# Cross-attention on one core: probability casts behind two score tiles in the filling slots, last value stores on GpSimd's queue, and the last normalization and value pass moved in the end

## The chip, the cores and the metric

The kernel runs on one core of one Trainium2 chip. The metric is the device time of one execution in microseconds (us). Before the change it is 1960.85 us, the median of 3 runs (1959.88 to 1962.95).

## What is computed

The reference, cut to what matters. `x` is (32, 512, 640), `ctx_2048` is (32, 77, 1024), all float32, 20 heads of 32 columns. The other three attention branches of the reference read context rows beyond the 77th, of which there are none, so they add nothing.

```python
q = _heads(hidden_states @ to_q_w)
p = softmax(einsum('bhqd,bhkd->bhqk', q, k) / sqrt(32))   # k = _heads(ctx @ to_k_w)
h_txt = einsum('bhqk,bhkd->bhqd', p, v)                   # v = _heads(ctx @ to_v_w)
out = _merge(h_txt) @ to_out_w + to_out_b + residual
```

## The kernel before, in words

Every float32 operand of a matmul is split into a high part (a cast to float32r, on ScalarE, ACT in the profile) and a low part (a subtraction on VectorE, DVE, or on GpSimd, POOL), and each product is three matmuls on TensorE (PE): high by high, high by low, low by high.

**Stages.** First the keys and values of all 32 x 77 context rows are computed in groups of 512 rows and stored in DRAM as `k_dram` and `v_dram`. The last group has 416 rows (group `LAST`); its values are still being computed while the main loop begins. Then come 160 slots, one for each tile n = 5b + j of batch b and chunk j of four heads. At the end the function `end` closes the last batch.

**A slot.** Slot n does, in the order in which `slot` (lines 660 to 762) writes it down, the scores and exponentials of tile n (four score tiles t of 128 queries, each into one of 3 banks `sc`, with a maximum `nm` on DVE, line 461, and four ACT exponentials with their sums, line 471), the queries of tile n+1 (`pq`, line 434, split into `qt` by line 103 on ACT and line 104 on DVE), the normalization of tile n-1 (`rs`, line 481 on DVE; `pn`, line 486 on POOL), its transposition (`z`, line 493 on DVE), the stores of `z` to DRAM (four DMAs `pd`, line 500), the load of tile n-2 in the layout that the value pass needs (`raw`, two DMAs, lines 509 and 510), and the value pass of tile n-3: `cast_p` (line 517, ACT, 128x1024), `rest_p` (line 523, ACT, 64x512, and line 524, DVE, 128x1024), `last_p` (line 531, POOL, 64x512), six matmuls `pa` (line 545), `sum_a` (line 556 on ACT into `aw`, two sums in line 558 on DVE), and one slot later `high_a` (line 565, ACT) and `low_a` (line 570, DVE), which give `at`. The output projection of an earlier batch (`po`, line 588, in pieces that `piece` deals out) and its sum with bias and residual (`finish`, line 617, DVE, and a DMA) fill the rest of PE's time.

**What sets the order.** Each engine works its instructions off in the order of the program text; nothing is rescheduled. A DMA waits in the queue of the engine that issues it (SP for nearly all), and keeps what is behind it waiting. A tile with one buffer (`z`, `pp`, `aw`, `pa`) or two or three (`raw`, `sc`, `po`) is written again only when its last reader is done; for `z` that is the landing of the four `pd` stores.

**Filling slots.** A slot is called filling if it has a value pass (n of 3 and more) but no output projection yet: slots 3 to 6. In slots 0 and 1 the last value chunks of group `LAST` are computed beside the scores: chunks 0 and 1 come ahead of slot 0, chunk 2 in slot 0, chunks 3 and 4 in slot 1. `split_values` (line 221) writes them to one of two buffers `vs` and stores each with four DMAs on SP (line 233).

**The end.** In slot 159 nothing is ahead. Its last lines take the value pass of tile 156 with `take` (line 641: `values`, `sum_a`, `high_a`, `low_a`). `end` (line 764) then takes tiles 157, 158 and 159 (N-3, N-2, N-1), normalizes tile 159, transposes, stores and loads it, and begins eight output banks of the last batch: banks 0 to 2 are `sc` banks, 3 the `pq` bank, 4 and 5 the `po` banks, 6 and 7 halves of the `pa` bank. `begin(i, j0, j1)` adds the products of chunks j0 to j1-1 to bank i, three matmuls each, and `close(t)` adds chunk 4, which needs the `at` of the last tile, to the two banks of row tile t and finishes them.

Of the kernel before, what the change touches and what calls it, by code (L numbers as in the profile page):

```python
# [51 lines left out]
def kernel(  # L52
# [25 lines left out]
    nc = tc.nc  # L78
# [8 lines left out]
    N = B * NC_  # L87
# [133 lines left out]
    def split_values(g, j, between=None):  # L221

        g0, gn = GROUPS_KV[g]
        na = gn // Q
        vs = vss[j % 2]
        vt = vs[:, :na, 2].bitcast(F32)
        nc.vector.transpose(vt, pvs.pop(j)[:, :gn].rearrange("p (a d) -> p a d", d=HD))
        if between is not None:
            between()
        split(vs[:, :na, 0], vs[:, :na, 2], vt)  # L230
        dst = v_dram[g0 : g0 + gn, :, j].rearrange("(a t) i c d -> i t a (c d)", t=Q)
        for i in range(HPC):
            nc.sync.dma_start(
                dst[i].bitcast(F32),
                vs[i * Q : (i + 1) * Q, :na].rearrange("p a c d -> p a (c d)").bitcast(F32),
            )
# [73 lines left out]
    LAST, split_ks = len(GROUPS_KV) - 1, []  # L310
# [155 lines left out]
    def exps(n, t, sc, nm):  # L466
        if t == 0:
            sms[n] = main.tile([P, NQ * HPC], F32, tag="sm", name="sm", bufs=2)
        for i in range(HPC):
            at = t * HPC + i  # L470
            nc.scalar.activation(  # L471
                pnb[n % 2][:, at, :NKEY],
                sc[:, i * NKEY : (i + 1) * NKEY],
                AF.Exp,
                bias=nm[:, i : i + 1],
                accum_out=sms[n][:, at : at + 1],
            )
# [133 lines left out]
    def finish():  # L611

        while closed:
            b, t, h = closed.pop(0)
            xr = xrs[b, t]
            cols = slice(h * HALF, (h + 1) * HALF)
            nc.vector.tensor_tensor(  # L617
                xr[:, cols], pos.pop((b, t, h))[:, :HALF], xr[:, cols], ALU.add
            )
            if (b, t) == (B - 1, NQ - 1):  # L620
                nc.sync.dma_start(out[b, t * P : (t + 1) * P, cols], xr[:, cols])
            elif h == 1:
                nc.sync.dma_start(out[b, t * P : (t + 1) * P, :], xr)
# [17 lines left out]
    def take(m):  # L641
        values(m)
        sum_a(m)
        high_a(m)
        low_a(m)
# [14 lines left out]
    def slot(n, beside=()):  # L660
        b, j = divmod(n, NC_)
        ahead, more = n + 1 < N, b + 1 < B
        back, first = PIECES[j]
        bo_, has_out = b - back, b >= back
        xsplits = SPLIT_X.get(j, ((), ())) if more and n > LATE else ((), ())
        turns = TRANSPOSE_X.get(j, ((), (), ())) if more and b else ((), (), ())
        if b == 1 and j < 2:
            turns = (((), (), ()), ((0, 1), (2,), ()))[j]
        taken = takes.get(n)

        filling = taken is not None and not has_out
        if not filling:
            refill(b, j, 0)
        if taken is not None:
            cast_p(taken)
        if n - 1 in takes:
            high_a(takes[n - 1])
        s = scores(n, 0)
        if taken is not None:
            rest_p(taken)  # L680
        rs = sums(n - 1) if n else None
        if taken is not None:
            last_p(taken)
        if n:
            normalize(n - 1, rs)
        if n - 1 in takes:
            low_a(takes[n - 1])
        exps(n, 0, *s)
        if ahead:
            queries(n + 1, 0, 2)  # L690
        s = scores(n, 1)
        if n - LAG + 1 in pds and n > LATE:
            load_p(n - LAG + 1)
        if filling:
            refill(b, j, 0)
        if n == NC_:
            load_x(b + 1, (2, 3))
        for k in WO.get(n, ()):
            nc.sync.dma_start(wos[0][:, k].bitcast(F32), wo_dram[:, k].bitcast(F32))
        refill(b, j, 1)  # L700
        finish()
        if j == 4 and b and b + 2 < B:
            load_x(b + 2, (0, 1))
        if j in RESIDUAL and b >= RESIDUAL[j][0]:
            load_residual(b - RESIDUAL[j][0], RESIDUAL[j][1])
        if j in BIAS and b >= BIAS[j][0]:
            add_bias(b - BIAS[j][0], BIAS[j][1])
        exps(n, 1, *s)
        for i in turns[0]:
            transpose_x(b + 1, i)  # L710
        if ahead:
            queries(n + 1, 2, NC_)
        s = scores(n, 2)
        if not ahead:
            exps(n, 2, *s)
            piece(bo_, first)
            s = scores(n, 3)
        if j == 3 and has_out:
            piece(bo_, first)
            finish()  # L720
        if n and has_out:
            transpose_p(n - 1)
        if ahead:
            split_q(n + 1)
            exps(n, 2, *s)
        if n and not has_out:
            transpose_p(n - 1)
        if j == 4 and b + 2 < B:
            load_x(b + 2, (0, 1) if not b else (2, 3))
        for c in xsplits[0]:  # L730
            split_x(b + 1, c)
        if not ahead:
            exps(n, 3, *s)
            finish()
            piece(bo_, first + 1)
            take(taken)
            return
        if has_out:
            if j != 3:
                piece(bo_, first)  # L740
        else:
            s = scores(n, 3)
        if taken is not None:
            values(taken)
        if len(beside) > 0:
            context_values(LAST, beside[0], psv)
        if has_out:
            s = scores(n, 3)
        finish()
        for i in turns[1]:  # L750
            transpose_x(b + 1, i)
        if taken is not None:
            sum_a(taken)
        for c in xsplits[1]:
            split_x(b + 1, c)
        exps(n, 3, *s)
        if len(beside) > 1:
            context_values(LAST, beside[1], psv)
        if has_out:
            piece(bo_, first + 1)  # L760
        for i in turns[2]:
            transpose_x(b + 1, i)

    def end():


        last = B - 1
        load_p(N - 2)
        cast_p(N - 3)
        rest_p(N - 3)  # L770
        last_p(N - 3)
        normalize(N - 1, sums(N - 1))
        add_bias(last - 1, 3)
        piece(last - 1, 6)
        finish()
        piece(last - 1, 7)
        finish()
        transpose_p(N - 1)
        load_p(N - 1)
        load_residual(last, 0)  # L780
        load_residual(last, 1)
        piece(last - 1, 8)
        take(N - 3)
        piece(last - 1, 9)
        cast_p(N - 2)
        rest_p(N - 2)
        last_p(N - 2)
        finish()
        spare = late[0].tile([P, 3, S], F32, tag="raw", name="xr", bufs=2)
        load_residual(last, 3, spare.rearrange("p k q -> p (k q)")[:, :C])  # L790
        load_residual(last, 2)

        def begin(i, j0, j1):
            t, h = divmod(i, 2)
            if j0 == 0:
                if i < 3:
                    pos[last, t, h] = ps.tile([P, S], F32, tag="sc", name="po", bufs=3)
                elif i == 3:
                    pos[last, t, h] = ps.tile([P, S], F32, tag="pq", name="po", bufs=1)
                elif i < 6:  # L800
                    output_bank(last, t, h)
                else:
                    if i == 6:
                        pas[N] = late[1].tile([P, 2, S], F32, tag="pa", name="po", bufs=1)
                    pos[last, t, h] = pas[N][:, i - 6]
            for j in range(j0, j1):
                project(last, t, h, j)

        begin(0, 0, 2)
        begin(1, 0, 2)  # L810
        take(N - 2)
        cast_p(N - 1)
        rest_p(N - 1)
        last_p(N - 1)
        for t in (0, 1, 3, 2):
            add_bias(last, t)
        begin(2, 0, 3)
        begin(0, 2, 4)
        begin(1, 2, 4)
        begin(2, 3, 4)  # L820
        for i in range(3, 6):
            begin(i, 0, 4)
        take(N - 1)

        def close(t):
            for h in range(2):
                project(last, t, h, 4)
                closed.append((last, t, h))
            finish()

        begin(6, 0, 4)
        close(0)
        close(1)
        begin(7, 0, 4)
        close(2)
        close(3)

    load_keys(0, 0)
# [63 lines left out]
```

## Time and profile before

| | |
|---|---|
| median of 3 runs | 1960.85 us (1959.88 to 1962.95) |
| the profiled execution: its own time, its span | 1961.89 us, 1959.8 us |
| granted PE clock, mean | 0.992 |
| PE busy | 1909.2 us, 97% of the span |
| ACT, DVE, POOL busy | 78%, 73%, 51% |
| HBM traffic over the span | 219 GB/s |

The span runs from the first to the last instruction; all times within it count from its start. A line of the timeline gives start, duration, engine, line of the kernel, operation, and in brackets how long the engine had been idle ahead of it and what ended that idle time. A line of the windows gives the stretch, its length, the busy time of PE, PEld (weight loads), DVE, ACT and POOL with the number of instructions, the granted PE clock, the busy share of the DMA engines and GB/s. PEq, SPq and the like are the queues of instructions that issue or wait and are not counted as busy. Idle time on an engine that is not the bottleneck costs nothing.

### The profile page before, as it was taken

Reading aid. Unit: us, or ns where it says so; the run is one execution under the profiler, and the core shown is the slowest. Engines: PE = TensorE matmul, PEld = TensorE weight load, DVE = VectorE, ACT = ScalarE, POOL = GpSimd, SP = SyncE. Lnnn points to the kernel's source line nnn. Section 1 sums busy time; section 2 is a strip of 40 time slices with the busy share of each in tenths; the row PEclk is TensorE's granted clock in tenths of the full one; section 3 lists DMA queues with packets and bytes.
Section 4 is the critical chain, followed back from the end, with each engine's and each line's share of the span. In section 5 each row is a group of like instructions: output and inputs, shape, how many; then the busy total and the mean of one; then the engine's idle time right before and its main releaser. Section 6 shows DMA issues by size and latency. Waiting matters only on the chain.

```text
span 1959.8 us, 36241 instructions
## 1 busy us (share of the span) xinstructions
PE 1909.2 (97%) x10332; PEld 1704.8 (87%) x10332; DVE 1436.2 (73%) x2334; ACT 1534.3 (78%) x6210; POOL 1002.3 (51%) x648
## 2 busy tenths in 40 slices
PE   9999997899999999999999999999999999999997
PEld 7787896798988989989999988889989998988896
DVE  4444345778788888888888777787878878878774
ACT  3232237888889888888888888899888988888982
POOL 1000033655566555555556555666556665566643
PEclk9999998999999999999999999999999999999999
DMA  9878869888888888888998888888898888888874
GB/s 187 185 182 234 197 159 238 219 226 226 226 229 234 223 234 232 231 228 222 235 236 230 230 212 238 229 235 223 226 235 231 226 228 226 226 226 228 226 212 135
DMA packets 568279, 431.28 MB, mean 220 GB/s; under 512 B 195344, under 2 KB 477072, under 8 KB 568080
## 3 DMA queue, kind: packets, MB, share of 16 engines
q1 hardware_dynamic: 564848, 417.65, 83.0%
q0 software_dynamic: 3136, 11.14, 1.6%
q8 instruction: 84, 1.38, 0.3%
q14 instruction: 115, 0.94, 0.2%
q10 hardware_dynamic: 96, 0.16, 0.0%
HBM read 247.17 MB, written 181.64 MB: 219 GB/s over the span
## 4 chain that ended last, share of the span: by engine, by line
PE 21%; DMA 19%; issue 17%; ACT 16%; DVE 12%; POOL 11%; SPq 3%; DVEq 0%; POOLq 0%; ACTq 0%
DMA raw<-pd 8%; ACT pn L471 8%; DMA pd<-z 8%; POOL pn L486 7%; PE pq L434 6%; PE po L588 6%; POOL pp L531 3%; DVE pp L524 3%; PE pv L191 3%; PE sc L453 2%; PE pk L191 2%; ACT xt L262 2%; ACT aw L556 2%; DVE nm L461 2%; DVE z L493 2%
## 5 line engine op out<-in xcount | busy, mean ns | idle before, releaser
L471 ACT ACTIVATE pn<-sc,nm 128x77 f32<-128x77 f32 x2560 | 802.6, 335 | 76.6 <-DVE nm L461 74.3
L588 PE MATMUL po<-wo_s,at 128*128 128x320 f32 x3840 | 626.0, 311 | 21.5 <-DVE xr L617 14.2
L434 PE MATMUL pq<-xt,wq_s 128*128 128x512 f32 x2400 | 605.7, 393 | 0.0
L588 PEld LDWEIGHTS po<-wo_s,at 128*128 128x128 f32 x3840 | 576.6, 189 | 32.2 <-DVE xr L617 24.6
L531 POOL TENSOR_TENSOR pp<-raw,pp 64x512 fp32r<-64x512 f32 x160 | 211.1, 1319 | 663.6 <-ACT pp L523 390.4
L471 ACT ACTIVATION_READ_ACCUMULATOR pn<-sc,nm 128x1 f32 x2560 | 545.2, 213 | 0.0
L434 PEld LDWEIGHTS pq<-xt,wq_s 128*128 128x128 f32 x2400 | 437.0, 188 | 75.2
L453 PE MATMUL sc<-kb,qt 128*128 128x308 f32 x1920 | 379.1, 306 | 13.9 <-ACT pn L471 10.4
L486 POOL TENSOR_TENSOR pn<-pn,rs 128x1232 f32<-128x1232 f32 x160 | 364.4, 2278 | 32.9 <-DVE rs L481 20.5
L453 PEld LDWEIGHTS sc<-kb,qt 128*128 128x128 f32 x1920 | 325.5, 189 | 59.3 <-ACT pn L471 12.3
L493 DVE STREAM_TRANSPOSE z<-pn 128x1280 f32<-128x1280 f32 x160 | 241.8, 1512 | 176.1 <-POOL pn L486 166.7
L461 DVE TENSOR_REDUCE nm<-sc 128x4 f32<-128x308 f32 x640 | 294.5, 462 | 41.3 <-PE sc L453 39.2
L524 DVE TENSOR_TENSOR pp<-raw,pp 128x1024 fp32r<-128x1024 f32 x160 | 195.5, 1222 | 91.8 <-ACT pp L517 86.7
L545 PE MATMUL pa<-pp,vb 128*128 128x512 f32 x960 | 253.3, 399 | 1.6 <-DVE pp L524 0.8
L558 DVE TENSOR_TENSOR pa<-pa,aw 64x512 f32<-64x512 f32 x320 | 222.7, 696 | 31.5 <-ACT aw L556 22.2
L263 POOL TENSOR_TENSOR xt<-xs,xt 128x512 fp32r<-128x512 f32 x160 | 204.4, 1296 | 37.8 <-ACT xt L262 36.9
L556 ACT COPY aw<-pa 64x1024 f32<-64x1024 f32 x160 | 162.0, 1013 | 69.5 <-PE pa L545 66.7
L545 PEld LDWEIGHTS pa<-pp,vb 128*128 128x128 f32 x960 | 175.3, 189 | 32.2 <-DVE pp L524 1.1
L517 ACT CAST pp<-raw 128x1024 fp32r<-128x1024 f32 x160 | 168.8, 1055 | 43.2 <-DMA raw<-pd 43.0
L581 POOL TENSOR_TENSOR xr<-xr,bias 128x640 f32<-128x640 f32 x128 | 201.6, 1576 | 0.1
L191 PE MATMUL pk<-ct,wk_s 128*128 128x512 f32 (+1 forms) x600 | 140.5, 394 | 8.2 <-ACT ct L103 6.3
L191 PEld LDWEIGHTS pk<-ct,wk_s 128*128 128x128 f32 x600 | 116.2, 195 | 30.8 <-ACT ct L103 7.2
(42 smaller groups left out, 1347.0 us busy)
## 6 DMA issues: line engine op xcount, KB each, us to landing
pd<-z SPq DMA_DIRECT2D x640, 160.0 KB, 3.9
raw<-pd SPq DMA_DIRECT2D x160, 512.0 KB, 4.0
xs<-in_x_dram SPq DMA_DIRECT2D x128, 320.0 KB, 6.2
xr<-in_x_dram SPq DMA_DIRECT2D x128, 320.0 KB, 4.1
out_dram<-xr SPq DMA_DIRECT2D x127, 320.0 KB, 4.1
raw<-pd SPq DMA_DIRECT2D x160, 128.0 KB, 4.2
v_dram<-vs SPq DMA_DIRECT2D x80, 192.0 KB, 3.9
k_dram<-ks POOLq DMA_DIRECT2D x20, 512.0 KB, 3.4
```

The source lines that it names most:

```text
L191: nc.tensor.matmul(held[j][:, :gn], w[:, k, a, :], cts[g, k][:, c, :gn], start=(k == 0 and n == 0), stop=(k == NK - 1 and n == 2),)
L434: nc.tensor.matmul(pqs[n], wq_s[:, k, a, j * P : (j + 1) * P], xts[b, k][:, c, :], start=(k == 0 and m == 0), stop=(k == NC_ - 1 and m == 2),)
L453: nc.tensor.matmul(sc[:, :KCOLS], qt[:, a, t * P : (t + 1) * P], kb[:, j - GROUPS[g][0], c], start=(m == 0), stop=(m == 2),)
L461: nc.vector.tensor_reduce(nm, sc[:, :KCOLS].rearrange("p (h k) -> p h k", k=NKEY), AX.X, ALU.max, negate=True)
L471: nc.scalar.activation(pnb[n % 2][:, at, :NKEY], sc[:, i * NKEY : (i + 1) * NKEY], AF.Exp, bias=nm[:, i : i + 1], accum_out=sms[n][:, at : ...
L486: nc.gpsimd.tensor_tensor(pf, pf, rs.unsqueeze(2).to_broadcast([P, NQ * HPC, NKEY]), ALU.mult)
L493: nc.vector.transpose(z.rearrange("p b t j -> p t b j"), pn.rearrange("p (t h) k -> p t (h k)", t=NQ).rearrange("p t (b i) -> p t b i", i=Q),)
L524: nc.vector.tensor_tensor(pp[:, 2:4, :], raw[:, 0:2, :], pp[:, 0:2, :].bitcast(F32), ALU.subtract)
L531: nc.gpsimd.tensor_tensor(pp[64:, 4, :], raw[:64, 2, :], pp[:64, 4, :].bitcast(F32), ALU.subtract)
L545: nc.tensor.matmul(pas[n][:, p, :], vb[:, p, t, :], pp[:, c, :], start=(c == p), stop=(t == 1),)
L558: nc.vector.tensor_tensor(pa[64 * p : 64 * p + 64, 0], pa[:64, p], aw[:, p], ALU.add)
L588: nc.tensor.matmul(pos[b, t, h][:, :HALF], ats[b * NC_ + j][:, a, t * P : (t + 1) * P], wos[0][:, j, c, h * HALF : (h + 1) * HALF], start= ...
```

## The change

1. The 20 DMAs that store the values of group `LAST` are issued by GpSimd, no longer by SP. In POOL's queue the stores of chunk 2 stand ahead of the normalization of tile 0, and those of chunks 3 and 4 ahead of that of tile 1.
2. In slots 3 to 6 the casts of the probabilities (`cast_p`, `rest_p`, `last_p`) come after the exponentials of score tiles 0 and 1. On ACT two tiles of exponentials stand ahead of them; on DVE the subtraction `pp` stands behind the reciprocal and the maximum of score tile 1 and ahead of the maximum of score tile 2; on POOL `pp` comes after the normalization.
3. In slot 159 the reciprocal and the normalization of tile 159 come directly after its last exponentials, and `end` begins with the transposition of tile 159 and its four stores, ahead of `high_a` and `low_a` of tile 156. On DVE `z` thus stands ahead of `at`, `pp` and the two sums `xr` that it followed before. On SP its stores stand ahead of an output store. On POOL the normalization comes ahead of `pp` of tile 157.
4. The value pass of the last tile is taken after bank 3, ahead of banks 4 and 5 (24 matmuls); banks 6 and 7, which lie in the `pa` bank, come behind `close(1)` and `close(2)`.

No instruction is added or removed on any engine, apart from the DMAs that change their queue.

```diff
         dst = v_dram[g0 : g0 + gn, :, j].rearrange("(a t) i c d -> i t a (c d)", t=Q)
+        engine = nc.gpsimd if g == LAST else nc.sync
         for i in range(HPC):
-            nc.sync.dma_start(
+            engine.dma_start(
...
-        if taken is not None:
+        if taken is not None and not filling:
             cast_p(taken)
...
         s = scores(n, 0)
-        if taken is not None:
+        if taken is not None and not filling:
             rest_p(taken)
         rs = sums(n - 1) if n else None
-        if taken is not None:
+        if taken is not None and not filling:
             last_p(taken)
...
         exps(n, 1, *s)
+        if filling:
+            cast_p(taken)
+            rest_p(taken)
+            last_p(taken)
         for i in turns[0]:
             transpose_x(b + 1, i)
...
             exps(n, 3, *s)
+            normalize(n, sums(n))
             finish()
             piece(bo_, first + 1)
-            take(taken)
+            values(taken)
+            sum_a(taken)
             return
...
         load_p(N - 2)
+        transpose_p(N - 1)
+        high_a(N - 4)
+        low_a(N - 4)
         cast_p(N - 3)
         rest_p(N - 3)
         last_p(N - 3)
-        normalize(N - 1, sums(N - 1))
         add_bias(last - 1, 3)
...
         finish()
-        transpose_p(N - 1)
         load_p(N - 1)
...
-        for i in range(3, 6):
-            begin(i, 0, 4)
+        begin(3, 0, 4)
         take(N - 1)
+        begin(4, 0, 4)
+        begin(5, 0, 4)
...
-        begin(6, 0, 4)
         close(0)
         close(1)
+        begin(6, 0, 4)
+        close(2)
         begin(7, 0, 4)
-        close(2)
         close(3)
```

## The prediction

> **What bounds the kernel now.** I read the page first (PE busy 97% of 1959.8 us), then the waits of PE by stage, the windows by slot, and the timelines of the two places that the change touches. From 420 to 1900 us PE waits 10.3 us in all, every one for `xr L617`, which the change leaves alone: a steady slot of 10.1 us is PE's. So the loop gives nothing, and what PE loses before and after it is lost for good.
>
> The fill is slots 3 to 7. The windows, one slot each (PE, PEld, DVE, ACT, POOL, clock, DMA share, GB/s):
>
> ```profile
> 304.18:318.03 13.85, 8.76 (x34) 7.06 (x35) 6.16 (x10) 8.82 (x45) 4.01 (x2) 0.82 0.84 219
> 318.03:326.71 8.68, 7.70 (x34) 6.17 (x32) 5.83 (x11) 8.45 (x33) 6.84 (x5) 0.90 0.97 260
> 326.71:338.55 11.84, 7.97 (x34) 6.07 (x34) 7.50 (x12) 9.14 (x42) 4.00 (x3) 0.93 0.78 193
> 338.55:348.49 9.94, 8.42 (x38) 6.65 (x36) 8.65 (x15) 8.77 (x40) 3.57 (x3) 0.91 0.99 204
> 348.49:361.58 13.09, 10.64 (x57) 9.19 (x58) 9.80 (x15) 11.43 (x46) 7.20 (x5) 1.00 0.65 172
> ```
>
> No engine fills slots 3, 5 or 7; slot 4 is ACT's (8.45 of 8.68). The timeline of the fill shows why:
>
> ```profile
> 300.82 5.51 SPq L233 DMA_DIRECT2D v_dram<-vs  x8
> ...
> 306.38 0.52 SPq L509 DMA_DIRECT2D raw<-pd  x1
> ...
> 311.69 1.04 ACT L517 CAST pp<-raw 128x1024 fp32r<-128x1024 f32 x1 [3.68 <-DMA raw<-pd]
> ...
> 314.53 1.14 PE L453 MATMUL sc<-kb,qt 128*128 128x308 f32 x3 [4.90 <-ACT pn L471]
> ...
> 336.11 0.69 PE L453 MATMUL sc<-kb,qt 128*128 128x308 f32 x3 [3.44 <-ACT pn L471]
> ...
> 359.44 1.51 DVE L493 STREAM_TRANSPOSE z<-pn 128x1280 f32<-128x1280 f32 x1 [2.86 <-POOL xr L581]
> ...
> 361.58 0.41 PE L453 MATMUL sc<-kb,qt 128*128 128x308 f32 x1 [2.15 <-DVE qt L104]
> ```
>
> In slot 3 the cast stands in ACT's queue ahead of the exponentials, and waits for a load that SP issued behind eight value stores; PE waits 4.90 us for the bank those exponentials free. In slot 7 the transpose `z` of DVE is late (POOL's `pn` had long ended; the stores `pd` issued from 353.46 for 3.55 us, last out of `z`, are what ended it) and `qt` behind it holds PE 2.15 us.
>
> The timeline of the end:
>
> ```profile
> 1911.95 2.21 SPq L500 DMA_DIRECT2D pd<-z  x4
> ...
> 1917.36 0.38 SPq L509 DMA_DIRECT2D raw<-pd  x1
> ...
> 1917.80 4.19 PE L588 MATMUL po<-wo_s,at 128*128 128x320 f32 x18 [2.97 <-DVE xr L617]
> ...
> 1920.75 1.51 DVE L493 STREAM_TRANSPOSE z<-pn 128x1280 f32<-128x1280 f32 x1 [2.61 <-POOL pn L486]
> ...
> 1941.51 1.56 PE L545 MATMUL pa<-pp,vb 128*128 128x512 f32 x6
> ...
> 1947.03 8.85 PE L588 MATMUL po<-wo_s,at 128*128 128x320 f32 x48 [3.96 <-DVE at L570]
> ```
>
> After the last value pass (1941.51) PE has nothing it may do until `at` is split at 1946.97; 24 matmuls that could run there were run before it.
>
> **Part 1: last values stored by GpSimd.** 20 DMAs leave SP, 20 join POOL's queue. The sources of two rows bracket the issue:
>
> ```profile
> L113 POOL DMA_DIRECT2D wraw<-in_L_xattn_to_v_w_dram x8: 498/498/688, 3.4 to 7.0; - x8
> L212 POOL DMA_DIRECT2D k_dram<-ks x20: 727/727/752, 50.9 to 221.5; - x20
> L233 SPq DMA_DIRECT2D v_dram<-vs x100: 302/730/2020, 54.9 to 305.5; - x100
> ```
>
> 498 ns is for 32 runs of 2,560 B, 727 for 256 runs; these stores have 32x13 = 416 runs of 384 B, which on a straight line is 0.89. SP took up to 2.02 for the same store. I take 0.8, near 727, and keep 0.5 and 2.02. The first three chunks cost nothing: POOL stood idle 8.91 us ahead of 287.44. Chunk 4 is ready at 300.6; its four issues end at 303.8, and only then comes the normalization of tile 1, queued behind them (301.32 before). It ends at 306.1, `z` at 307.65 (306.27 before), the next maximum `nm` at 308.1, so the last exponentials of slot 2 start at 308.1 instead of 306.67: **+1.4 us**, inside what follows. For SP: `pd` of tile 0 follows `z` at 292 to 294 instead of 296.01, and the load of tile 0 goes out near 299 instead of 306.38. With its 5 us to land (306.4 to 311.6 above) that is 304, so the 3.68 us wait goes. If the load were late after all, only casts and `qt` would wait, no longer the exponentials.
>
> Row and rule: POOL's 20 `k_dram` issues stayed within 727 to 752 ns while DVE was busy 44 to 46% (21.6 to 22.8 of 49 us from 49 to 196 us). The Trainium skill, page "SBUF — State Buffer", section "SBUF: two separate sides", speaks against this part: descriptors of a GpSimd DMA can't be written while DVE holds the shared port, and a 620 ns DMA took about 3100 ns beside such a copy. By 3.1 us each, my estimate from that page, the normalization would start 17 us later and the kernel would be slower; the row argues otherwise.
>
> **Part 2: casts behind two score tiles (slots 3 to 6).** No instruction is added. On ACT a tile of exponentials is 1.21, cast 1.05, second cast 0.5, `qt` 0.5, `aw` 1.0, `at` 0.5 (starts to starts). Slot 3: three tiles from 308.1 end at 311.75, the cast at 312.8, DVE's `pp` (1.23) at 314.05, and `nm` of tile 2, now queued behind it, at 314.5. Call this point T. The value pass needs POOL's `pp` at about 315, so the next slot's scores start near 315.7 against 318.03: -2.3.
> From T on the loop is ACT and DVE in turn: `qt` 0.65, `z` 1.5, `nm` 0.45 (T+2.6), exponentials 1.21, `at` 0.5 (the sums on DVE end at T+4.05), two tiles 2.4, cast 1.05, `pp` 1.25, `nm` 0.45: 9.75 us, against 8.68 and 11.84 in slots 4 and 5. Here a new wait costs: ACT sits 0.7 us per slot for the `nm` behind `pp`. T4 is 10.95 later (three `xt` casts), T5 9.75, T6 9.75 plus 1.57 for two transposes of x that stand between: 346.5. `qt` is ready at 347.2, slot 7's scores end at 347.6 against 348.91: **-1.3**. In slot 7 `pd` of tile 5 goes out at about 349, not behind a later `z` and eight value loads at 353.46, so the 2.86 us wait of `z` becomes a wait for POOL: `qt` is ready at T6+11.7 = 358.2, and PE, 11.0 us of its own work after 347.6, meets it at 358.6. PE's 2.15 us go, less what is late: -1.6 more. Fill: **-2.9 us**, kept by a PE-bound loop. With 0.5 us per issue -4.1; each 0.1 us above 0.8 takes 0.4 back, 0.8 from 1.1 on, where chunk 3 (ready 296.1) backs up too.
>
> **Part 3: the end.** Moved sooner: reciprocal, POOL's 2.28 us normalization (POOL idle after 1911.9), DVE's `z` and its four `pd` issues. `z` now stands ahead of `at` (0.69), `pp` (1.23) and `xr` on DVE. It may not overwrite `z` before tile N-2's `pd` stores have landed; SP's load that waits for the same stores went out at 1917.36. So `z` runs 1917.35 to 1918.85, `at` to 1919.5, `pp` to 1920.7, `xr` to 1921.2, and PE, which waits for that bank, resumes at 1921.2 instead of 1917.80: **+3.4**. The chain behind (`pa`, `aw`, sums, `at`, cast, twice) shows no slack, so all of it moves. SP's queue has the output store of row tile 2 between; the last `raw` load then goes out near 1924 and lands by 1928, needed at 1937: covered.
> Then the gain. `pa` of the last tile starts at 1938.0 + 24 x 0.152 = 1941.7 (`pp` ready 1937.25 + 3.4 = 1940.65), no later than before though all else slipped. Split `at` is ready 5.46 later, at 1947.15; PE fills 3.65 of it with banks 4 and 5, so it is not cold: 48 matmuls x 0.152 = 7.3 instead of 8.85. PE ends at 1954.5 against 1955.88, and the row tile stored before the last leaves 0.4 sooner: -1.75. The longer early wait costs clock, which these windows price:
>
> ```profile
> 1917.80:1920.00 2.20, 2.20 (x8) 2.20 (x9) 0.34 (x1) 0.00 (x0) 2.12 (x2) 0.50 0.67 80
> 1949.00:1951.00 2.00, 2.00 (x10) 2.00 (x9) 0.25 (x1) 0.00 (x0) 0.00 (x0) 0.50 0.00 0
> ```
>
> A 3.0 us wait was followed by at least 2.2 us at half clock, worth 1.1; after some 6 us of waiting I allow 0 to 1.1 more, value 0.5. (The Trainium skill, "TensorE: Matmul & The Clock Gate", Part 1, has a free-running window of about 3.4 us; a wait of 6 us always spans one, a wait of 3 only by luck, so by it nothing more is lost here.) End: **-1.2 us** (+0.8 to -2.2).
>
> **Sum**: -2.9 - 1.2 = -4.1. The profiled execution (span 1959.8, 1961.89 in all) lies 1.0 above the median of runs, 1960.85; I take the difference from the median: **1956.8 us**.
>
> **Rivals.** *All of the end* (0.13): `z` does not hold DVE, because the `pd` stores land by 1914. Then nothing slips by 3.4, PE ends at 1951.1 and the tail 0.4 sooner: -5.2, and 1952.7 in all. For: POOL is free. Against: SP's own wait till 1917.36. *Fill given back* (0.20): an issue costs 1.1 to 1.33, the fill nets -1.7 to 0, time 1958 to 1959.7. For: 416 short runs. Against: 727 ns flat. *Slower* (0.10): POOL's issue costs what SP's slowest did, 2.02. Chunks 3 and 4 then hold POOL till 300.6 - 4.5 + 8 x 2.02 = 312.3, 8.5 later than I have it: fill +5.6, end -1.2, 1965.2. It decides against the change above 1.33 us an issue.
>
> **How the numbers follow.** My forecast has 0.57, its own range 1954 to 1959. A measurement of this kernel can tell 0.2% (3.9 us) from no change; that bound cuts my case nearly in half: 0.36 faster, 0.21 within. With the first rival, faster 0.49; with the second, within 0.41; slower 0.10. The range takes in the first rival and the second with the end at its worst: 1952.5 to 1961.
>
> **What would show it.** Right: no wait of 3 us or more of PE for `pn L471` in slots 3 to 6; the casts wait for DMA under 1 us; slots 4 and 5 near 9.8 each; at the end a PE wait of about 6 us for `xr`, and none of 4 us for the last `at`. Wrong: POOL's stores above 1.1 us each, `z` of the last tile starting before 1916, or a steady slot off 10.1 us.

## The result and the profile after

In the first comparison, six runs of each kernel, the changed kernel takes **1952.32 us** (median; 1951.64 to 1955.12) against 1961.58 (1959.88 to 1962.95): ratio 0.9957, 95% interval 0.9944 to 0.997. Two further comparisons, told below, gave 0.9981 (0.997 to 0.9992) and 0.9979 (0.9964 to 0.9994). So the change makes the kernel faster, by 0.2 to 0.4%. Its size was 8 us in the first comparison (1961.58 x 0.0043, medians 9.3 apart) and 4 in the other two.

I cut each profile into four stretches: *ahead* (to the first score tile), *fill* (from there to the start of slot 10), *loop* (to PE's 18 `po` matmuls behind slot 159's third score tile) and *end*. Between the two first profiles, spans of 1959.8 and 1949.9, the 9.9 us lie so: ahead 2.31, fill 3.11, loop 3.17, end 1.31. The change touches only the second and the fourth.

In the changed kernel lines 232 to 708 are one higher (L471 is L472, L617 is L618). GpSimd's stores, from the answer on their source line (duration minimum, median and maximum, first and last start):

```profile
L234 POOL DMA_DIRECT2D v_dram<-vs x20: 642/642/692, 270.3 to 300.5; - x20
```

The fill in the timeline of after, PE alone:

```profile
307.99 0.69 PE L454 MATMUL sc<-kb,qt 128*128 128x308 f32 x3 [0.54 <-ACT pn L472]
310.20 0.47 PE L546 MATMUL pa<-pp,vb 128*128 128x512 f32 x1 [1.52 <-POOL pn L487]
311.41 2.40 PE L546 MATMUL pa<-pp,vb 128*128 128x512 f32 x5 [0.74 <-DVE pp L525]
...
321.00 0.49 PE L546 MATMUL pa<-pp,vb 128*128 128x512 f32 x1 [1.44 <-ACT pp L518]
...
356.01 0.41 PE L454 MATMUL sc<-kb,qt 128*128 128x308 f32 x1 [0.29 <-DVE qt L104]
```

The waits of 4.90 and 3.44 us for a score bank are gone, and `qt`'s of 2.15 is 0.29; in their place PE waits 1.2 to 1.5 and then 0.75 us for `pp` in each of slots 3 to 6 (slot 3's first wait, 1.52, is put down to POOL's `pn`, which stands ahead of POOL's `pp`): the value passes now wait, not the scores. The windows of the same slots (columns as before the change; the cuts are the starts of the slots' scores):

```profile
301.87:313.61 11.74, 8.76 (x34) 6.26 (x34) 7.00 (x10) 8.71 (x45) 5.60 (x3) 0.91 0.75 214
313.61:324.56 10.95, 8.75 (x34) 6.98 (x33) 7.18 (x13) 9.62 (x40) 7.77 (x5) 0.81 0.80 211
324.56:334.38 9.82, 7.65 (x35) 5.88 (x34) 6.40 (x12) 8.67 (x37) 4.04 (x2) 0.97 0.93 200
334.38:344.74 10.36, 8.12 (x34) 6.40 (x33) 7.57 (x13) 7.81 (x32) 4.02 (x2) 0.88 0.88 175
344.74:355.28 10.54, 10.54 (x59) 9.61 (x58) 9.13 (x14) 10.21 (x45) 5.12 (x3) 0.96 0.65 175
```

The end in the timeline of after:

```profile
1908.64 1.51 DVE L494 STREAM_TRANSPOSE z<-pn 128x1280 f32<-128x1280 f32 x1 [2.81 <-DMA pd<-z]
1908.65 0.38 SPq L510 DMA_DIRECT2D raw<-pd  x1
...
1910.07 0.65 DVE L571 TENSOR_TENSOR at<-pa,at 128x512 fp32r<-128x512 f32 x1
1910.65 1.34 DVE L525 TENSOR_TENSOR pp<-raw,pp 128x1024 fp32r<-128x1024 f32 x1
...
1911.91 0.87 DVE L618 TENSOR_TENSOR xr<-po,xr 128x320 f32<-128x320 f32 x2
1912.44 4.42 PE L589 MATMUL po<-wo_s,at 128*128 128x320 f32 x18 [6.10 <-DVE xr L618]
...
1932.87 1.55 PE L546 MATMUL pa<-pp,vb 128*128 128x512 f32 x6
1934.26 11.13 PE L589 MATMUL po<-wo_s,at 128*128 128x320 f32 x72
```

`z` waits 2.81 us for the landing of the stores of tile N-2 and stands ahead of `at`, `pp` and `xr`; PE, which needs the bank that `xr` frees, is idle 6.10 us instead of 2.97. Behind the last value pass PE runs 72 matmuls without the wait of 3.96.

### The profile page after: what moved, and what is told of

Read it like the earlier page. It is cut to its first block, busy times and chain, and to the rows that moved or that the text cites. A ratio compares the mean times of both kernels' runs of the same rounds, so it can differ in the third digit from the quotient of the medians.

```text
span 1949.9 us, 36251 instructions
## 1 busy us (share of the span) xinstructions
PE 1905.3 (98%) x10332; PEld 1701.3 (87%) x10332; DVE 1437.6 (74%) x2334; ACT 1533.9 (79%) x6210; POOL 1015.2 (52%) x668
## 4 chain that ended last, share of the span: by engine, by line
PE 20%; ACT 19%; issue 17%; DMA 15%; DVE 13%; POOL 12%; SPq 2%; DVEq 0%; POOLq 0%; ACTq 0%
ACT pn L472 10%; POOL pn L487 8%; DMA raw<-pd 7%; DMA pd<-z 6%; PE pq L435 5%; PE po L589 5%; POOL pp L532 4%; DVE pp L525 3%; ACT xt L263 3%; ACT aw L557 3%; PE pk L191 2%; PE pv L191 2%; PE sc L454 2%; DVE nm L462 2%; DVE z L494 2%
## 5 line engine op out<-in xcount | busy, mean ns | idle before, releaser
L472 ACT ACTIVATE pn<-sc,nm 128x77 f32<-128x77 f32 x2560 | 802.5, 335 | 70.9 <-DVE nm L462 68.0
L472 ACT ACTIVATION_READ_ACCUMULATOR pn<-sc,nm 128x1 f32 x2560 | 545.1, 213 | 0.0
```

Of the source, the lines that this page charges most:

```text
L472: nc.scalar.activation(pnb[n % 2][:, at, :NKEY], sc[:, i * NKEY : (i + 1) * NKEY], AF.Exp, bias=nm[:, i : i + 1], accum_out=sms[n][:, at : ...
```

## The experiments

The question was twofold: where the other 5 us came from (ahead 2.3, loop 3.2), and which part of the change earns what. The later runs were made on four chips, each with its own runs of the kernel before (medians 1956.47, 1957.57, 1959.10 and 1956.68), so ratios are to be compared, not times. All four stretches of all profiles, in us; in brackets behind the loop the sum of PE's waits in it:

| profile of | ahead | fill | loop (waits) | end |
|---|---|---|---|---|
| before, first | 274.47 | 107.07 | 1520.46 (11.26) | 57.80 |
| before, again | 272.16 | 107.01 | 1515.18 (5.77) | 57.75 |
| after, first | 272.16 | 103.96 | 1517.29 (8.06) | 56.49 |
| after, again | 271.11 | 104.47 | 1517.04 (7.48) | 58.18 |
| after, third | 270.72 | 104.01 | 1517.88 (8.27) | 59.09 |
| stores alone | 273.09 | 102.09 | 1514.28 (4.86) | 60.24 |
| casts alone | 273.30 | 107.62 | 1515.07 (5.29) | 59.61 |
| end alone | 274.71 | 107.35 | 1514.96 (5.37) | 58.18 |
| order of banks alone | 274.31 | 108.32 | 1515.17 (5.19) | 54.20 |
| after, maximum first | 271.52 | 103.83 | 1519.89 (9.91) | 58.56 |
| stores and order | 273.09 | 102.29 | 1518.85 (9.38) | 54.87 |
| ... and ready work first | 273.92 | 103.79 | 1515.05 (5.51) | 51.74 |
| ... and added matmuls | 272.98 | 104.01 | 1516.31 (6.63) | 50.20 |
| stores, order, casts behind one tile | 271.77 | 105.80 | 1517.88 (8.04) | 53.25 |

**1. Both kernels again.** No edit. Expected of the kernel before:

> The kernel before, unchanged, a second time. The two profiles differ by 9.9 us in span: 2.3 of it lies ahead of the first score tile (274.47 against 272.16 us), in a stage that the change does not touch, 3.1 in the fill, 3.2 in the steady loop, 1.3 at the end. Theory S (the sum): the change is worth about 4.4 us (fill and end); the other 5.5 are differences between executions of one and the same kernel. By it this profile has its first score tile anywhere between 272 and 275 us, and its loop (start of slot 10, to PE's 18 matmuls after the last slot's third score tile) anywhere between 1517.3 and 1520.5 us, with several runs below 1959. Rival K (knock-on): the change shifts the clock's and the loop's luck for good; then this profile repeats the before's numbers: first score tile at 274 to 275, loop 1520 to 1521, and the median stays at 1961 to 1962.

And of the changed one, twice:

> The changed kernel, unchanged, a second time. Theory S: median 1952 to 1957 and a first score tile or a loop that differs from the first profile's (272.16; 1517.3 us) by a us or more in either direction. Rival K: median 1952 to 1953 again, first score tile within 0.5 us of 272.16, loop within 0.5 us of 1517.3.

> The changed kernel a third time, since its gain was 0.43% of the time in the first comparison (6 runs each) and 0.19% in the second (12 runs against 35). Theory S: fill 103.9 to 104.5 and end 56.4 to 58.6 once more, hence a gain of some 4.2 us, ratio 0.9975 to 0.9985; the first comparison's further 4 to 5 us are runs of the kernel before with a long loop. Rival K (the first comparison is the typical one): ratio 0.996 or below, with a first score tile before 272.2 and a loop under 1517 again.

Measured: before again 1958.17 (12 runs) beside 1956.47 for itself (35 runs), ratio 1.0005 (0.9994 to 1.0016); those 35 runs spread from 1950.53 to 1961.91. After: 1953.54 and 1953.50 (12 runs each) against 1956.47 (35) and 1956.68 (17), the two later ratios above. The second profile of before is 2.3 us shorter ahead (272.16) and 5.3 in the loop (1515.18), without the change. Rival K falls in the profiles: the loop is 1514.3 to 1520.5 us in kernels whose loop is the same code, and loop less PE's waits is 1509.2 to 1510.0 in all fourteen, so the whole spread is how often and how long `xr` is late (8 to 17 waits of up to 1.6 us). The loop of the first profile of before is the longest of all. Theory S is not met in three things: before again has a loop of 1515.18, under the 1517.3 that it gave; the third end of after, 59.09, is over its 58.6; and the three loops of after lie within 0.9 us of each other, though other kernels' lie on both sides. Why `xr` is late more often in one execution than in another was not tried. The stage ahead, the same code in all, is 270.7 to 274.7. One piece of it, from the timelines of before, first, and of after:

```profile
71.43 27.05 PE L191 MATMUL pk<-ct,wk_s 128*128 128x512 f32 x105 [3.09 <-ACT ct L103]
```

```profile
70.44 0.50 PE L191 MATMUL pk<-ct,wk_s 128*128 128x512 f32 x1 [2.88 <-ACT ct L103]
71.17 23.91 PE L191 MATMUL pk<-ct,wk_s 128*128 128x512 f32 x104 [0.23 <-DVE ct L104]
```

The same 105 matmuls behind a like wait (3.09 and 2.88 us) took 27.05 us there and 24.64 here: in before the four us from 71.43 show a granted clock of 0.50, in after the four from 71.17 show 1.00. What theory S does not explain either is that all six first runs of before are above 1959.8 and all six of after below 1955.2; why that comparison showed twice the difference of the other two stays open.

**2. The stores alone.** On the kernel before:

```diff
+        engine = nc.gpsimd if g == LAST else nc.sync
...
-            nc.sync.dma_start(
+            engine.dma_start(
```

> The kernel before with part 1 alone: the last group's values are stored by GpSimd; casts and end as before. Theory S: the load of tile 0 leaves SP near 297 instead of 306, the cast's wait of 3.68 us for it goes, but the cast still stands ahead of slot 3's exponentials, so PE's wait of 4.90 shrinks to some 2.5, and slot 5's of 3.44 stays or halves. Fill -2 us (0 to -3.5), time 1957 to 1961. Rival C (the casts carry the fill): no gain in the fill, within 0.5 us. Rival K: 1955 or below, since the stage ahead and the loop move too.

Measured: 1954.17 against 1956.47, ratio 0.9987 (0.9977 to 0.9998). The fill is 102.09, five us less than before and two less than with the whole change; the three later kernels with the same fill code have 102.29, 103.79 and 104.01. The load of tile 0 leaves SP at 296.51 and no cast waits for it. PE's waits for banks in slots 3 to 6, from the timeline of this kernel:

```profile
310.36 0.69 PE L454 MATMUL sc<-kb,qt 128*128 128x308 f32 x3 [1.97 <-DMA pd<-z]
...
320.56 0.69 PE L454 MATMUL sc<-kb,qt 128*128 128x308 f32 x3 [1.58 <-ACT pn L472]
...
329.56 0.69 PE L454 MATMUL sc<-kb,qt 128*128 128x308 f32 x3 [1.57 <-ACT pn L472]
...
339.72 1.08 PE L454 MATMUL sc<-kb,qt 128*128 128x308 f32 x3 [2.72 <-ACT pn L472]
...
355.18 0.41 PE L454 MATMUL sc<-kb,qt 128*128 128x308 f32 x1 [1.44 <-DVE qt L104]
```

The mechanism of theory S holds (the wait of 4.90 is 1.97, put down here to the stores `pd`), and the fill gains more (3.4 to 5.3 against the old code's mean of 107.44) than the 2 that it gave; rival C falls. The times set beforehand, 1957 to 1961 for theory S and 1955 or below for rival K, decide nothing, since the kernel before took 1956.47 in this comparison. By run times alone the gain is 2.5 us (0.4 to 4.5), and 0.9987 can't be told from the whole change's 0.9981 and 0.9979: that the stores carry the fill rests on the stretches.

**3. The casts alone.** On the kernel before:

```diff
-        if taken is not None:
+        if taken is not None and not filling:
             cast_p(taken)        # so too rest_p, last_p
...
         exps(n, 1, *s)
+        if filling:
+            cast_p(taken); rest_p(taken); last_p(taken)
```

> The kernel before with part 2 alone: in slots 3 to 6 the casts stand behind two score tiles' exponentials; stores on SP, end as before. Theory S: the load of tile 0 still leaves at 306.4 and lands at 311.6, so the cast waits over 1 us for it, but no longer holds the exponentials: PE's waits for exponentials in slots 3 to 6 fall under 1 us each, and the value passes wait instead. Fill -2 to -3 us, time 1957 to 1960. Rival P (the stores carry the fill): gain under 0.5 us. Rival K: 1955 or below.

Measured: 1956.12 against 1956.47, ratio 0.9998 (0.9989 to 1.0008); fill 107.62. Rival P holds, theory S with its 2 to 3 us falls: the casts by themselves earn nothing. The load still leaves at 305.24, the cast waits 1.71 us for it, and what no longer holds the scores holds the value passes: PE waits 3.26 us for slot 3's (the row names no releaser), and in slot 8 it waits 2.22 for `qt` as before:

```profile
312.15 0.77 PE L545 MATMUL pa<-pp,vb 128*128 128x512 f32 x1 [3.26 <-issue]
```

One window from slot 3's first scores to slot 8's, 20 score tiles with the same work in every kernel, shows how near each kernel comes to the work of ACT, the busiest engine. Before, after and the stores alone, in this order:

```profile
304.18:358.98 54.80, 43.04 (x189) 34.96 (x190) 35.80 (x56) 45.01 (x195) 23.07 (x14) 0.91 0.85 211
```

```profile
301.87:355.28 53.41, 43.82 (x190) 35.14 (x191) 37.28 (x57) 45.02 (x196) 26.54 (x15) 0.90 0.80 196
```

```profile
302.81:353.30 50.49, 41.40 (x190) 32.71 (x191) 36.05 (x57) 45.19 (x196) 25.12 (x16) 0.97 0.81 206
```

ACT works 45.0 to 45.2 us in all three (fourth pair); the stretch is that plus what ACT stands idle: 9.8, 8.4 and 5.3. The stores take 4.5 us of idle time away, and the moved casts put 3.1 of them back. The other profiles agree: 54.8, 53.4, 54.9 and 54.3 us in the four with the old code, 53.4, 53.9 and 53.0 in the three of after, 50.5, 50.4, 49.9 and 50.1 in the four with the stores and the old place of the casts, 55.25 in the one with the casts alone. What the casts return is slot 8: its wait for `qt`, 1.44 to 2.15 us with the stores alone, is 0.24 to 0.65 in after, and with it goes a loss of clock (1.6 us behind that wait of 2.15 in the two profiles of experiment 8). Over the whole fill the means are 104.15 (after, three profiles) and 103.05 (stores and old casts, four): the casts cost about 1 us on top of the stores, but the samples touch: what is shown is the 3 us in slots 3 to 7, and for the whole fill only that the casts bring no gain on top.

**4. The end alone, and only its order.** The first has all of part 3 and 4 of the change. The second has part 4 alone:

```diff
-        for i in range(3, 6):
-            begin(i, 0, 4)
+        begin(3, 0, 4)
         take(N - 1)
+        begin(4, 0, 4)
+        begin(5, 0, 4)
...
-        begin(6, 0, 4)
         close(0)
         close(1)
+        begin(6, 0, 4)
+        close(2)
         begin(7, 0, 4)
-        close(2)
```

> The kernel before with part 3 alone: early normalization and early transpose z of the last tile, value passes of the last tile ahead of banks 4 and 5. I measure the end from PE's 18 matmuls behind the last slot's third score tile to the end of the span: 57.8 and 57.75 us in two executions of before, 56.5 and 58.2 in two of after. Theory Z (z holds DVE): PE waits about 6.1 us for xr behind z and the end lasts 56.5 to 58.2, 0 to 1.3 better than before. Rival F (z is free): that wait stays at 3.0 and the end lasts 53.

> The kernel before with one piece of part 3 alone: the value passes of the last tile ahead of the matmuls of banks 4 and 5, and bank 6 behind two row tiles' last matmuls; normalization and z of the last tile stay where they were. Theory Z: the early normalization buys nothing here, since the last tile's load lands long before its cast; so the wait for xr is 3.0, the value passes of the last tile start 3.65 us sooner, PE runs 72 matmuls without a stop behind them, and the end lasts 52.3 (51.5 to 54, with what the clock takes after waits), 5.5 better than before and 4 better than with the early z. Rival N (the early normalization is needed): the value passes wait for pp and the end lasts 55.5 or more.

Measured against 1957.57: the end alone 1956.96, 0.9997 (0.9987 to 1.0007), end 58.18, wait for `xr` 6.10; the order alone 1952.76, **0.9968 (0.9957 to 0.998)**, end 54.20, wait 2.98. From the timelines of the end alone, and of the order alone:

```profile
1916.05 5.17 PE L588 MATMUL po<-wo_s,at 128*128 128x320 f32 x18 [6.10 <-DVE xr L617]
```

```profile
1913.59 4.44 PE L588 MATMUL po<-wo_s,at 128*128 128x320 f32 x18 [2.98 <-DVE xr L617]
...
1935.59 1.56 PE L545 MATMUL pa<-pp,vb 128*128 128x512 f32 x6
1936.98 3.96 PE L588 MATMUL po<-wo_s,at 128*128 128x320 f32 x26
1941.11 7.01 PE L588 MATMUL po<-wo_s,at 128*128 128x320 f32 x46 [0.16 <-DVE at L570]
```

The last value pass starts early without the early normalization too. So theory Z's mechanism holds: the early normalization and `z` are pure cost, some 4 us (58.10, the mean of five ends with all of parts 3 and 4, against 54.1, the mean of three with the order alone), and the order alone is worth 4.7 (58.85, the mean of four ends with the old code, to 54.1). Its size does not: 54.20 is over the range of 51.5 to 54. Clock can be the reason: the 22 matmuls ahead of the last value pass took 5.04 us here, against 3.50 in experiment 6, whose end with the same order is 53.25. Rival N, with 55.5 or more, falls.

**5. The maximum first.** The changed kernel, with DVE's `pp` behind the third maximum (in these slots the transposes of x that followed `last_p` stay behind it):

```diff
         if filling:
             cast_p(taken)
-            rest_p(taken)
-            last_p(taken)
...
         s = scores(n, 2)
+        if filling:
+            rest_p(taken)
+            last_p(taken)
```

> The changed kernel, but in slots 3 to 6 DVE takes the maximum of the third score tile ahead of the subtraction pp (it stood behind it), nothing else moved. I measure the fill from the first score tile to the start of slot 10: 107.07 and 107.01 us in before, 103.96 and 104.47 in after, 102.09 with the stores alone, 107.62 with the casts alone. Theory M (the maximum queued behind pp is what the moved casts cost): ACT's waits of 0.7 us for nm in slots 3 to 6 go, the casts come 0.7 sooner per slot, and the fill lasts 101 to 102.5. Rival A (the moved cast is simply later, by two tiles of exponentials, and the value passes with it): ACT's wait goes but the slot stays bound elsewhere; fill 103.5 to 104.5.

Measured: 1952.55 against 1957.57, 0.9972 (0.9962 to 0.9983), which the changed kernel's own intervals take in; fill 103.83. Theory M falls, rival A holds. ACT's waits of 0.7 us for `nm` are gone, and ACT waits instead for the value pass, ahead of `aw`; in slots 4 and 5, where it waited 0.89 and 0.25 in after, the timeline of ACT has

```profile
323.82 1.01 ACT L557 COPY aw<-pa 64x1024 f32<-64x1024 f32 x1 [1.61 <-PE pa L546]
...
334.22 1.01 ACT L557 COPY aw<-pa 64x1024 f32<-64x1024 f32 x1 [1.69 <-PE pa L546]
```

By these waits the bound is now the round from the cast over `pp` and the value pass to `aw`; no run shortened a step of it.

**6. Casts behind one tile**, with stores and order: the three calls directly behind `exps(n, 0)`.

> The kernel with stores by GpSimd and the value passes ahead of banks 4 and 5, with the casts of slots 3 to 6 behind one score tile's exponentials instead of ahead of all of them (0 tiles: fill 102.09 and 102.29) or behind two (103.96, 104.47). Theory A (ACT bounds the fill with the same 45.0 us of work in slots 3 to 7 in all kernels; what its order makes it stand idle is the fill's length): one tile earlier than two, pp is ready before PE has done its score tiles, ACT neither waits for nm nor for the value passes, and the fill is 101 to 102.5. Rival B (every tile that the cast is set back costs 1 us): 103 to 103.5.

Measured: 1950.82 against 1959.10, 0.9957 (0.9941 to 0.9973); fill 105.80. Both were wrong, in this one profile it is the worst of the three places: DVE's `pp` now stands ahead of the second tile's maximum, and ACT waits for it in each of slots 3 to 6, as in its timeline of ACT:

```profile
321.86 0.33 ACT L472 ACTIVATE pn<-sc,nm 128x77 f32<-128x77 f32 x1 [1.19 <-DVE nm L462]
...
332.10 0.33 ACT L472 ACTIVATE pn<-sc,nm 128x77 f32<-128x77 f32 x1 [1.18 <-DVE nm L462]
```

That wait makes slots 3 to 7 no longer than in after (53.5 us against 53.0 to 53.9); the rest of the 105.80 is slot 8, where PE waits 1.99 us for `qt`, as with the casts ahead. By run times it can't be told from experiment 7 below (0.9957 and 0.9958).

**7. Stores and order together.** The edits of 2 and 4's second kernel.

> The kernel before with the values stored by GpSimd and the last tile's value passes ahead of banks 4 and 5; casts, normalization and z of the last tile as before. Theories S and Z together: fill 102.1 as with the stores alone (-5), end 52.3 (-5.5); time 10 us below before's median on this chip, ratio 0.995, and 6 to 7 us below the changed kernel. If the end is not free of z's place (rival N), 4 to 5 us below before only.

Measured: 1949.48 against 1957.57, 0.9958 (0.9943 to 0.9974): 8 us, for a promised 10; fill 102.29, end 54.87 instead of 52.3, of which 1.5 is clock (22 matmuls in 5.04 us). That is below the changed kernel's two later ratios by 0.2%, some 4 us instead of the 6 to 7 promised, with intervals that touch.

**8. Ready work first, and matmuls that nothing reads.** On 7, ahead of `take(N - 1)`:

```diff
         begin(2, 0, 3)
-        begin(0, 2, 4)
-        begin(1, 2, 4)
-        begin(2, 3, 4)
-        begin(3, 0, 4)
+        begin(0, 2, 3)
+        begin(1, 2, 3)
+        begin(3, 0, 3)
+        for i in range(4):
+            begin(i, 3, 4)
         take(N - 1)
```

> The kernel with stores by GpSimd and the value passes ahead of banks 4 and 5 (ends of 54.2 and 54.9 us with that order), and one more change of order at the end: behind the value passes of tile N-2 PE first does all that is ready (chunks 0 to 2 of banks 0 to 3, 24 matmuls), and only then the 12 matmuls of chunk 3, which wait for tile N-2's at. Theory W (PE's waits at the end cost their own length and, in most executions, some 1.5 us of half clock behind them): the 1.47 us wait for at goes, and with it the 1.5 us that its 22 matmuls lost (5.04 instead of 3.50); the last value passes start when pp is ready, some 3.3 us behind the split at instead of 5.6; end 52 to 53. Rival D (the chain through DVE sets the end, whatever PE does): end 54 to 55.

The second kernel adds, ahead of the matmuls that wait for `xr`, 16 like this into a free `sc` bank:

```diff
+            nc.tensor.matmul(spin[:, :HALF], ats[last * NC_][:, 0, :P],
+                             wos[0][:, 0, 0, :HALF], start=True, stop=True)
```

> As the kernel with all that is ready first, with 16 matmuls added that nothing reads, into a free bank, in the wait of 2.98 us for xr. Theory W: PE's wait falls to some 0.6 us, the 18 matmuls behind it take 2.8 to 3.3 instead of 4.45, and the end is 1 to 1.6 us shorter than without them. Rival G (the clock falls on its own count of time, not for the wait): the 18 matmuls take 4.2 to 4.5 again and the end is the same, or longer by what the added matmuls overrun.

Measured against 1959.10: 1946.92, **0.994 (0.9924 to 0.9955)**, end 51.74 (the value passes start 1.6 us behind the split `at`, sooner still than said; rival D falls); and 1946.05, **0.9934 (0.9916 to 0.9951)**, end 50.20. Both beat the kernel before and, by their intervals, the changed one's two later comparisons; between the two, the intervals do not tell. The windows behind the wait for `xr`, one us each, without the added matmuls and with them (the third number from the right is the clock):

```profile
1908.54:1909.54 1.00, 1.00 (x7) 1.00 (x8) 0.34 (x1) 0.00 (x0) 0.92 (x2) 1.00 0.68 92
1909.54:1910.54 1.00, 1.00 (x7) 1.00 (x7) 0.00 (x0) 0.00 (x0) 1.00 (x1) 0.71 0.67 195
1910.54:1911.54 1.00, 1.00 (x5) 1.00 (x5) 0.05 (x1) 0.00 (x0) 1.00 (x2) 0.50 0.98 376
1911.54:1912.54 1.00, 1.00 (x5) 1.00 (x5) 1.00 (x1) 0.00 (x0) 1.00 (x1) 0.50 0.83 313
1912.54:1913.54 1.00, 1.00 (x5) 0.76 (x4) 0.46 (x1) 0.00 (x0) 0.43 (x1) 0.58 0.02 8
```

```profile
1909.08:1910.08 1.00, 1.00 (x7) 1.00 (x8) 0.33 (x1) 0.00 (x0) 0.92 (x2) 1.00 0.10 32
1910.08:1911.08 1.00, 1.00 (x9) 1.00 (x8) 0.00 (x0) 0.00 (x0) 1.00 (x1) 1.00 1.12 84
1911.08:1912.08 1.00, 1.00 (x9) 0.95 (x8) 0.05 (x1) 0.00 (x0) 1.00 (x2) 1.00 0.91 219
```

The wait of 2.96 us is followed by half clock; a wait of 0.62 is not, and the 18 matmuls take 2.90 instead of 4.01. The end is 1.54 us shorter. Theory W holds and rival G falls, by one profile with the added matmuls against eight without (last section).

## Why the prediction was right, and where it was not

**The sum was right.** -2.9 in the fill and -1.2 at the end: the profiles give -3.3 (107.44, the mean of four fills with the old code, to 104.15) and -0.75 (58.85 to 58.10, the mean of the five ends with all of parts 3 and 4), together -4.0 for a predicted -4.1. That it fits to 0.1 us is luck: the two parts miss by 0.4 and 0.45 in opposite directions, and the ends of the changed kernel alone spread from 56.49 to 59.09. The two later comparisons, 0.19% and 0.21% of 1957 us, say -3.7 and -4.1. That the first one's median came 4.5 us below 1956.8, a hair under the range, is no term of the sum: the profiled 5.5 us beyond it lie ahead of the change and in the loop, and what failed is the range, which had nothing in it for code that is the same.

**The issue cost** was 0.64 us, not 0.8. With the 0.4 us that the prediction gave for each 0.1, that makes its fill -3.5. The second rival and the slower one, from 1.1 us on, fall with it. (By the prediction's own sums the change stops paying near 1.46 us an issue, where its end of -1.2 is used up, not at 1.33.) The Trainium skill, "SBUF — State Buffer", "SBUF: two separate sides", has GpSimd's DMA starved while DVE runs a copy in a mode that takes both ports. Nothing like it showed in 20 stores of 642 to 692 ns, though beside the first four of them DVE was busy the whole time, with transposes:

```profile
270.25:272.85 2.60, 2.60 (x16) 2.55 (x16) 2.60 (x5) 0.23 (x1) 2.60 (x4) 1.00 0.58 134
```

DVE runs no copy in these kernels, so the page's own case is not seen here.

**The steps of the fill** hold but for one, once 2.31 us are added to after's times for the earlier start: the last exponentials of slot 2 start at 307.7 (predicted 308.1), slot 4's scores at 315.9 (315.7), slots 4 and 5 last 10.95 and 9.82 (10.95, 9.75), slot 7's scores end at 348.0 (347.6), slot 8's `qt` comes at 358.3 (358.6). The maximum behind `pp`, the prediction's T, starts at 311.27, 322.12, 332.53 and 343.80 us in after: the rounds are 10.85, 10.41 and 11.27 for 10.95, 9.75 and 11.32, so the one of slot 5 was 0.7 too short. The sign "slots 4 and 5 near 9.8 each" does not fit slot 4's 10.95, nor the prediction's own sum for it.

**What failed in the fill** is the step that priced parts 1 and 2 only together. "The 3.68 us cast wait goes" was part 1's doing, and part 1 without part 2 has 50.2 us for slots 3 to 7 (mean of four) where the two together have 53.5 (mean of three). I saw the new wait of ACT (0.7 us in slots 3 to 5, 2.15 in slot 6, where two transposes of x stand between) and booked it inside a gain, where it was a loss against the stores alone. The waits in slots 3 and 6 of after:

```profile
311.78 0.33 ACT L472 ACTIVATE pn<-sc,nm 128x77 f32<-128x77 f32 x1 [0.71 <-DVE nm L462]
...
344.27 0.33 ACT L472 ACTIVATE pn<-sc,nm 128x77 f32<-128x77 f32 x1 [2.15 <-DVE nm L462]
```

It was not even the whole loss: experiment 5 took that wait away, and the value pass's took its place.

**The end.** "+3.4" for `z` ahead of `xr`: measured 3.46 (the value pass of N-3 starts at 1916.70, 8.59 us being the lead of after at that point). The wait of 6 us came as 6.10, the last value pass at the predicted place (1932.87 + 8.59 = 1941.5 for 1941.7), the 72 matmuls without a stop. The clock took 0.25 more than before in the first two profiles (4.42 against 4.19 for the 18 matmuls), for an allowed 0.5; in other executions it is 4.57 to 5.17 behind the wait of 6.1 and 3.90 to 4.45 behind that of 3.0. The prediction's sentence from the Trainium skill does not follow: a wait is sure to hold one whole free-running window of 3.4 us only from 6.8 us on, one of 3.0 can hold none, and half clock came behind both. What the prediction did not have is 0.6 us at the very end: from PE's last matmul to the end of the span it is 3.9 to 4.0 us in the five profiles in which SP stores the last values, and 4.5 to 4.6 in the nine in which GpSimd does. So part 1 costs 0.6 there, where the prediction had 0.4 gained; no row says why. Without it, the ends give -1.1 for the predicted -1.2. The rival "all of the end" falls, but the kernel that it describes, order without the wait of 6 us, exists: it is part 4 alone, -4.7 for the rival's -5.2. I did not ask whether the early normalization was needed for the early value pass; `pp` ready at 1937.25 against a value pass possible at 1934.67 + 22 x 0.152 = 1938.0 stood in the same timeline.

## What to carry to other kernels

Price each part of a change against every other part, not only against the kernel before: here one queue move earned all of the fill, the reordering beside it brought no gain on top (in slots 3 to 7 it took 3 us back, in slot 8 and behind it returned 2), and a few moved lines at the end were worth more without the move they came with. Where in-order engines form a ring, moving a stall from one engine's wait to another's is no gain; add up what the busiest engine of the ring stands idle over the whole stretch. And before comparing two single profiles, cut them where the code is the same: half of the first difference lay there.

## What the runs showed of the hardware that I had not expected

Half clock comes in whole pieces of about 3.4 us and not at once: in the first windows above it begins 1.42 us after PE resumed and lasts 0.58 + 2 + 0.84 = 3.42 us (shares of a slice from its clock, 0.71 and 0.58). Behind the wait of 6.10 in after it is 3.38 us, with another 3.4 inside the wait (clock 0.72 over 6.10 us, so 0.56 of it at half). The Trainium skill, "TensorE: Matmul & The Clock Gate", Part 1, has free-running windows of about 3.4 us, and these rows agree with that. It asks for at least one idle window; here less was enough: 3.42 us back from the start of half clock, PE had been idle only 2.0 us of that piece and busy 1.42. In all eight profiles with a wait of about 3 us for `xr` and nothing in it, half clock followed, while behind the wait of 1.47 us the 22 or 46 matmuls took 3.50 or 7.00 us in four profiles and 5.03 to 5.05 or 8.54 to 8.56 in eight. So a wait of 1.5 us costs 0 or 1.5 more, and not always the same in one kernel: the three profiles of after have 3.50, 5.03 and 5.05.
